# Feed-forward statistics and roots one step later in a run, and one more bank left out

## The chip, the core and the metric

The kernel runs on one core of a Trainium2 chip. The metric is the device time of one execution in microseconds (us). Five engines work side by side, each in its own program order: TensorE (PE, with its weight loads as PEld), VectorE (DVE), ScalarE (ACT), GpSimd (POOL) and SyncE (SP), which issues the DMAs. They wait for one another by semaphores.

## The reference

The input x is 2 x 256 x 128 x 128 (batch, time, band, channel), all float32. Three residual blocks follow each other:

```
x = x + mha(ln(x) over times, causal mask, 4 heads)     # sequences of 256 times
x = x + mha(ln(x) over bands, |i - j| <= 16, 4 heads)   # sequences of 128 bands
x = x + gelu(ln(x) @ w1.T + b1) @ w2.T + b2             # 128 -> 512 -> 128
```

`ln` subtracts the mean over the 128 channels and multiplies by one over the root of variance + 1e-5. `mha` has 4 heads of 32 channels.

## The kernel before, in words

**Groups and steps.** The work is cut into groups of 4 x 128 tokens (512 columns). `groups` (lines 953 to 1020) yields first 128 `OverTime` groups, which leave their results in HBM, then, in 16 runs, 8 `OverBands` groups and 8 `FeedForward` groups each (RUN = 32 times, NT = 4 a group). A run's feed-forward groups take the band groups' results from SBUF. "Run" in this document is always this; what is measured is called an execution. I call the band groups and their steps B0 to B7, the feed-forward ones F0 to F7. `run` (line 1143) is one loop over steps n, one group a step, in which pieces of neighbouring groups are issued in an order written out by hand. Every engine keeps that program order: `InOrder` (line 867) pins each instruction, and since its helper at line 877 emits them, the profile has this one line for all.

**One group's way through the steps.** Mean and variance ("statistics", lines 383 to 390, VectorE: four `bn_stats` to tile stats, four `bn_aggr` to mv); "root" (lines 399 to 403, GpSimd: a small add and a power, to rstd); "normalize" (VectorE, xh) and "turn" (VectorE's transpose to z, then four DMAs to HBM) in the step three before its own; "fetch" of the turned tile (xnT) two before its own.

- A band group has queries, keys and values (wf products) made one step before its own. In its step: scores (qT,kT) into four PSUM banks; a minimum and an add of the band mask on the fourth head by VectorE; four exps on ScalarE to tile pf; six masks on GpSimd for the first three heads ("first_mask", line 784). One step later: "weigh" (line 798), which sums the weights (pf,ones, to bank rp) and weighs the values (pf,v, to op); "invert" on ScalarE; "divide" on VectorE, to oT. Two steps later: "output" (wn,oT, to yp) and "finish", VectorE's add into x.
- A feed-forward group has hidden products (xnT,w1f) and gelus in its step, then one step later weigh (w2T, to zp) and VectorE's add into res with the store.

In F0, called "turn" in the code, the inversion is an exact reciprocal on VectorE instead. In feed steps GpSimd adds biases (res, x), and statistics, roots and, at the end, products of the next run's band groups are made.

**Order around the change.** FeedForward root of group n + 4 is the first thing issued in step n (line 1182), ahead of that step's six masks on GpSimd. FeedForward statistics of n + 5 stand at the end of VectorE's step, after divide, in band steps and F0 (line 1253), and in the other feed steps before weigh, right after normalize and turn (line 1240). So F0's statistics are in B3, F3's in B6, F4's in B7, F7's in F2, each with the root a step later.

**PSUM banks.** In the runs `turn_of_bank` (line 913) hands out the eight banks in turn. A matmul into a bank waits until the last reader of what was in it is done. `weigh` of a band group first takes a bank for each name in `follow` and holds it for use later in the same step (line 801): "yp" for the output of the group before, "qp" for the queries of the group two after. B0 to B5 have both names, B6 and B7 only "yp" (lines 1159 to 1161). Weigh of B5 is in step B6, weigh of B6 in step B7.

Of the kernel before, what the change touches and what calls it, by code (L numbers as in the profile page):

```python
# [636 lines left out]
class OverTime(Attention):  # L637
# [5 lines left out]
    early, late = (1, 2), (0, 3)  # L643
# [238 lines left out]
class BoundedPath:  # L882
# [260 lines left out]
    def run(self, x, out):  # L1143
        groups = list(self.groups(x, out))

        def do(n, *names):
            if 0 <= n < len(groups):
                for name in names:
                    getattr(groups[n], name)()

        def at(n, kind):
            return 0 <= n < len(groups) and isinstance(groups[n], kind)

        def do_at(n, kind, *names):
            if at(n, kind):
                do(n, *names)


        for i in range(len(groups) - 2):
            if at(i, OverBands) and at(i + 2, OverBands):  # L1160
                groups[i].follow = ("yp", "qp")

        run0 = [i for i in range(len(groups)) if at(i, OverBands)][: RUN // NT]
        times = range(3 * NT, run0[-1] + 1)
        fours = {i + NT - 1: Four(self, groups[i : i + NT]) for i in times[::NT]}
        A = RUN // NT

        ff = [i for i in range(len(groups)) if at(i, FeedForward)][2:]

# [5 lines left out]
        for n in range(-12, len(groups) + 2):  # L1175
# [3 lines left out]
            old, new = (groups[i] if at(i, OverTime) else None for i in (n, n + 1))  # L1179
            if bands[2] and feeds[1]:  # L1180
                self.scalar.preload_act_table_set(EXP_SET)
            do_at(n + 4, FeedForward, "root")
            do(n, "first_half", "first_function", "first_mask")
            if n >= 0:
                if n + 5 < 3 * NT:
# [51 lines left out]
            if n < 0:  # L1237
                do(n + 5, "statistics")
            if not bands[2] and not turn:
                do_at(n + 5, FeedForward, "statistics")  # L1240
            if n == -5:
                self.fold_biases()
            do(n - 1, "weigh")
# [6 lines left out]
                self.bounded = self.nc.values_load(self.flag[0:1, 0:1], min_val=0, max_val=1)  # L1250
            do(n - 1, "divide")
            if bands[2] or turn:
                do_at(n + 5, FeedForward, "statistics")
            if not turn:
                do(n, "second_half", "second_function")
            if n in run0:
# [1 line left out]
            if not bands[2] and old is None:  # L1258
                do_at(n, FeedForward, "bias")
                do_at(n + A, OverBands, "bias")  # L1260
                if at(n - 1, FeedForward) and at(n - 2, OverBands):
                    do_at(n + A - 1, OverBands, "statistics", "root")
                if not turn:
                    do_at(n + A, OverBands, "statistics", "root")
            do_at(n + 2, OverTime, "queries_keys", "take_query", "take_key")
# [99 lines left out]
```

## Time and profile before

| what | value |
|---|---|
| median of 3 timed executions | 2655.34 us (2655.3 to 2656.77) |
| the profiled execution | 2659.84 us |
| its span, first to last instruction | 2658.1 us |
| mean granted TensorE clock | 0.997 |
| one run, from B0's first weigh to the next run's | 106.22 us in most runs |
| TensorE idle over the runs (934 us to the end), gaps over 0.03 us | 10.5 us |

The page gives for each engine busy time, its share of the span and the number of instructions. A row of a timeline has the start in us from the beginning of the span, the length, engine, line, operation, tiles out<-in with shapes, the number of like instructions merged, and in brackets the idle time of the engine just before and what ended it. The chain of work is followed back from the last instruction, at each step to what released it.

### The profile page before, as it was taken

Reading aid. Unit: us, or ns where it says so; the run is one execution under the profiler, and the core shown is the slowest. Engines: PE = TensorE matmul, PEld = TensorE weight load, DVE = VectorE, ACT = ScalarE, POOL = GpSimd, SP = SyncE. Lnnn points to the kernel's source line nnn. Section 1 sums busy time; section 2 is a strip of 40 time slices with the busy share of each in tenths; the row PEclk is TensorE's granted clock in tenths of the full one; section 3 lists DMA queues with packets and bytes.
Section 4 is the critical chain, followed back from the end, with each engine's and each line's share of the span. In section 5 each row is a group of like instructions: output and inputs, shape, how many; then the busy total and the mean of one; then the engine's idle time right before and its main releaser. Section 6 shows DMA issues by size and latency. Waiting matters only on the chain.

```text
span 2658.1 us, 156476 instructions
## 1 busy us (share of the span) xinstructions
PE 2629.9 (99%) x68694; PEld 1924.4 (72%) x68694; DVE 2135.9 (80%) x6423; ACT 1843.1 (69%) x3562; POOL 1951.8 (73%) x2302
## 2 busy tenths in 40 slices
PE   8999999999999999999999999999999999999998
PEld 5676676676676667777777787777776867777777
DVE  6888888888888887967868779678687796886874
ACT  6889889989989874664755746647557466475573
POOL 5999999999999986766667667666676676666762
PEclk9999999999999999999999999999999999999999
DMA  5556565556566444544444445444454444444533
GB/s 136 146 152 156 144 159 151 149 152 152 148 156 153 126 121 121 126 122 123 120 122 123 120 120 126 120 123 120 117 130 122 115 128 122 124 118 122 126 94 83
DMA packets 469781, 344.97 MB, mean 130 GB/s; under 512 B 43104, under 2 KB 404448, under 8 KB 469088
## 3 DMA queue, kind: packets, MB, share of 16 engines
q1 hardware_dynamic: 467696, 333.82, 49.9%
q8 instruction: 540, 8.85, 1.5%
q14 instruction: 153, 1.25, 0.2%
q10 hardware_dynamic: 1392, 1.06, 0.1%
HBM read 167.98 MB, written 166.72 MB: 126 GB/s over the span
## 4 chain that ended last, share of the span: by engine, by line
PE 86%; DVE 12%; issue 0%; DMA 0%; ACT 0%; POOL 0%; SPq 0%; ACTq 0%; DVEq 0%
PE bank L877 86%; DVE xh L877 3%; DVE bank L877 2%; DVE u L877 1%; DVE oT L877 1%; DVE z L877 1%; DVE stats L877 1%; DVE x L877 1%; DVE mv L877 0%; DMA xnT<-turned 0%; ACT p L877 0%; DMA f_wiT_sb<-in_f_wiT 0%; DMA turned<-z 0%; POOL rstd L877 0%; POOL pf L877 0%
## 5 line engine op out<-in xcount | busy, mean ns | idle before, releaser
L877 ACT ACTIVATE hT<-bank,b 128x512 f32<-128x512 f32 x512 | 346.9, 688 | 522.4 <-PE bank L877 494.4
L877 POOL TENSOR_SCALAR_AFFINE_SELECT pf<-pf 128x512 f32<-128x512 f32 x768 | 476.7, 635 | 176.2 <-ACT pf L877 150.0
L877 PEld LDWEIGHTS bank<-w2T_sb,hT 128*32 128x32 f32 x16384 | 494.5, 110 | 27.6 <-issue 20.9
L877 PE MATMUL bank<-xnT,w1f 128*32 128x512 f32 x4096 | 507.3, 592 | 0.0
L877 PE MATMUL bank<-w2T_sb,hT 128*32 128x128 f32 x16384 | 502.1, 273 | 0.5 <-issue 0.3
L877 PE MATMUL bank<-xnT,wf 128*32 128x512 f32 x4096 | 498.0, 596 | 4.6 <-ACT p L877 3.9
L877 ACT ACTIVATE p<-bank 128x512 f32<-128x512 f32 (+1 forms) x1024 | 430.4, 495 | 64.7 <-PE bank L877 64.6
L877 POOL TENSOR_SCALAR_AFFINE_SELECT p<-p 128x1024 f32<-128x1024 f32 (+2 forms) x384 | 364.0, 948 | 84.8 <-ACT p L877 76.4
L877 DVE TENSOR_SCALAR xh<-x,mv,rstd 128x160 f32<-128x160 f32 (+1 forms) x1040 | 403.1, 430 | 9.6
L877 PEld LDWEIGHTS bank<-wf,xnT 128*32 128x32 f32 x8192 | 247.5, 110 | 142.4 <-issue 102.7
L877 DVE TENSOR_TENSOR res<-bank,res 128x512 f32<-128x512 f32 x256 | 170.6, 666 | 217.5 <-PE bank L877 203.4
L877 PEld LDWEIGHTS bank<-xnT,w1f 128*32 128x32 f32 x4096 | 239.7, 110 | 132.5 <-issue 116.7
L877 POOL TENSOR_TENSOR p<-p,p 128x512 f32<-128x512 f32 x256 | 323.8, 1287 | 10.7
L877 DVE BATCH_NORM_STATS2 stats<-x 128x6 f32<-128x128 f32 x1536 | 329.7, 277 | 0.6 <-DMA f_woT_sb<-in_f_woT 0.6
L877 POOL TENSOR_SCALAR rstd<-mv 128x4 f32<-128x4 f32 x248 | 56.6, 228 | 369.8 <-DVE mv L877 369.1
L877 PE MATMUL bank<-qT,kT 32*64 32x80 f32 (+4 forms) x16384 | 304.4, 271 | 1.6 <-ACT p L877 1.1
L877 PEld LDWEIGHTS bank<-qT,kT 32*64 32x64 f32 x16384 | 261.1, 131 | 53.4 <-ACT kT L877 50.0
L877 ACT ACTIVATE pf<-bank 128x512 f32<-128x512 f32 x512 | 267.7, 602 | 42.5 <-PE bank L877 33.2
L877 PE MATMUL bank<-wn,oT 128*32 128x128 f32 x8192 | 287.4, 274 | 1.8 <-issue 0.8
L877 DVE STREAM_TRANSPOSE z<-xh 128x512 f32<-128x512 f32 x380 | 270.5, 712 | 13.5
L877 PE MATMUL bank<-wf,xnT 128*32 128x128 f32 x8192 | 279.2, 273 | 0.0
L877 POOL TENSOR_TENSOR rstd<-rstd,mhalf 128x4 f32<-128x4 f32 x248 | 257.6, 1039 | 20.7
(99 smaller groups left out, 3826.5 us busy)
## 6 DMA issues: line engine op xcount, KB each, us to landing
turned<-z SPq DMA_DIRECT2D x1520, 64.0 KB, 2.6
xnT<-turned SPq DMA_DIRECT2D x380, 256.0 KB, 3.1
x<-res SPq DMA_DIRECT2D x256, 128.0 KB, 2.3
x<-x SPq DMA_DIRECT2D x128, 256.0 KB, 4.2
out<-res SPq DMA_DIRECT2D x256, 128.0 KB, 2.3
x<-in_x SPq DMA_DIRECT2D x124, 256.0 KB, 4.4
x<-in_x SPq DMA_DIRECT2D x8, 64.0 KB, 3.3
x<-in_x SPq DMA_DIRECT2D x4, 128.0 KB, 3.8
```

The lines of the kernel that those rows point to most:

```text
L877: return self.tc.keep_in_program_order(emit(*args, **kwargs))
```

## The change

Two edits, both in `run`.

1. `follow` gets "qp" where the next group is a band group, not the one two after. That adds B6: its weigh, in step B7, takes a bank for queries that nobody uses, so the turn of banks skips one there.
2. The first three feed-forward groups of a run (`early`) keep statistics five steps and root four steps ahead. The other five have both four steps ahead, at the place in the step where statistics stood, root right behind. So F3's statistics go from B6 to B7, F4's from B7 to F0, F5's to F1, F6's to F2, F7's to F3; and their roots go from the head of the same step to a place behind those statistics.

```
-            if at(i, OverBands) and at(i + 2, OverBands):
+            if at(i, OverBands) and at(i + 1, OverBands):
                 groups[i].follow = ("yp", "qp")
...
+        early = [i for i in range(3, len(groups)) if at(i, FeedForward) and at(i - 3, OverBands)]
+
+        def statistics_of_feed(n):
+            if n + 5 in early:
+                do(n + 5, "statistics")
+            if at(n + 4, FeedForward) and n + 4 not in early:
+                do(n + 4, "statistics", "root")
...
-            do_at(n + 4, FeedForward, "root")
+            if n + 4 in early:
+                do(n + 4, "root")
...
             if not bands[2] and not turn:
-                do_at(n + 5, FeedForward, "statistics")
+                statistics_of_feed(n)
...
             if bands[2] or turn:
-                do_at(n + 5, FeedForward, "statistics")
+                statistics_of_feed(n)
```

No instruction is added or taken away.

## The prediction

> **What bounds the kernel now.** I read the page first, then the chain of work that ended last, then the timelines of TensorE, GpSimd and VectorE around one run (the sixth of the sixteen, 1485.16 to 1591.38 us), then the same places in all runs. All instructions carry the helper's line L877, so I go by tiles.
>
> ```profile
> PE 2629.9 (99%) x68694; PEld 1924.4 (72%) x68694; DVE 2135.9 (80%) x6423; ACT 1843.1 (69%) x3562; POOL 1951.8 (73%) x2302
> ```
>
> TensorE is busy almost throughout, but a matmul's recorded length says little, so I take the starts of like blocks. The page *Perfetto Trace Analysis* of the Trainium skill, section Identifying the Most-Contended Engine, speaks against reading this 99% as a limit: matmul busy time is no measure of distance to roofline, weight loads (here 72%) are a better one. If TensorE had such room in the band steps, all VectorE time freed there would be time won.
>
> ```profile
> 1509.20 1.06 PE L877 MATMUL bank<-pf,ones 128*32 128x512 f32 x8
> ...
> 1515.43 1.21 PE L877 MATMUL bank<-pf,ones 128*32 128x512 f32 x8
> ...
> 1520.91 0.97 PE L877 MATMUL bank<-qT,kT 32*64 32x80 f32 x64
> 1522.38 1.07 PE L877 MATMUL bank<-pf,ones 128*32 128x512 f32 x8 [0.50 <-DVE oT L877]
> ...
> 1528.41 1.33 PE L877 MATMUL bank<-pf,ones 128*32 128x512 f32 x8
> ```
>
> The block "pf,ones" opens weigh once a band step. Its pitch is 6.23 us (1502.97 for B4, then 1509.20 and 1515.43), in nearly every run and band step. From B6 to B7 it is 6.95. Between scores and weigh lie 0.90 us normally (1508.30 to 1509.20), here 1.47: a loss of 0.57 us in B7, which waits for VectorE's oT. VectorE meanwhile:
>
> ```profile
> 1510.78 1.05 DVE xh L877 x3
> ...
> 1517.33 1.04 DVE xh L877 x3
> ...
> 1521.54 0.70 DVE oT L877
> 1522.24 0.14 issue
> 1522.38 7.64 PE bank L877 x124
> ```
>
> This is the chain. VectorE's step is 6.54 us from B3 on, without a gap, against TensorE's 6.23. It falls behind 0.31 us a step until in B7 TensorE has to wait for it. So the row decides against the skill's rule: TensorE kept 6.23 while VectorE was slower and not yet in its way. By the rule the freed 1.06 us a run would give 17 us; by the row only what TensorE lost can come back.
>
> Why does weigh wait for oT? The banks: B7's four score banks, yp, then rp. Without a "qp" between, rp takes the bank of the op that divide of B5's group reads, last of all VectorE work of that step. In B1 to B6, with "qp" reserved, rp takes a key bank that ScalarE emptied in the step before.
>
> The third view is GpSimd's.
>
> ```profile
> 1518.15 3.93 POOL L877 TENSOR_SCALAR_AFFINE_SELECT pf<-pf 128x512 f32<-128x512 f32 x6
> 1523.38 0.23 POOL L877 TENSOR_SCALAR rstd<-mv 128x4 f32<-128x4 f32 x1 [1.29 <-DVE mv L877]
> 1523.69 1.04 POOL L877 TENSOR_TENSOR rstd<-rstd,mhalf 128x4 f32<-128x4 f32 x1
> 1524.70 3.93 POOL L877 TENSOR_SCALAR_AFFINE_SELECT pf<-pf 128x512 f32<-128x512 f32 x6
> ```
>
> Each step's six masks stand behind a root that waits for VectorE's late statistics (1.29 us of idle before it). The first row is the masks of B6, to 1522.08; the last those of B7. They end at 1528.63, while F0's weigh begins at 1528.41: its column groups of the third and fourth head start 0.28 us after the first two. That lag is carried through the feed steps (mixed rows) and paid at the next scores: the last two w2T blocks stand 9.10 us apart in runs with it, 8.88 in the one run whose lag was 0.04. It costs 0.22 us. A run of 106.22 us thus loses 0.57 + 0.22 = 0.79, sixteen some 12 us.
>
> **The change, part by part.**
>
> *The bank.* rp of B6's group moves to the bank of the keys (copied by 1520.74), op to that of the values (1521.61), the four hidden banks of F0 to the four score banks (last read by exp at 1524.51, needed about 1527), yp to the bank of the yp before (read by 1526.70, needed at 1530). All are free in time. Weigh may start at 1520.91 + 0.90 = 1521.81. But the mask of the third head ends at 1522.08; its root is F2's, which does not move. With 0.06 for the handoff (1528.63 to 1528.69) the late groups start at 1522.14, not 1522.38. So the oT wait is gone, and a new lag of 0.33 takes part of its place.
>
> *Root of F3 leaves the head of B7.* The masks of B7 start with exp at about 1522.6 instead of 1524.70 and end near 1526.5, before F0's weigh at 1528.2. The old lag of 0.28 is gone. Together: the late groups reach F0's weigh at 1522.14 + 6.03 = 1528.17 where they had 1528.69. Gain 0.52 us a run, if VectorE keeps up. Here the skill speaks against it: *GPSIMD Engine Reference*, section 8 (Key points), says that GpSimd shares its SBUF interfaces with VectorE, and contends with VectorE instructions in a two-port mode or with two SBUF inputs. The masks now lie beside normalizing (1.60 us); were they held up for all of that, they would end at 1528.1, still in time. The trace shows 0.63 to 0.64 us a mask beside "xh" or not, so I take nothing.
>
> *Statistics.* Four BATCH_NORM_STATS2 and four aggregates cost 1.06 us of VectorE's queue (1522.14 to 1523.20). B6 loses one set, F3 gains one; B7, F0, F1 and F2 keep one, of the group before. In F3 it is covered by the wait for zp, 2.94 us a step in the timeline from F4 on. In B7 VectorE runs 1.06 earlier: minimum at 1522.14 (scores are ready at 1521.95), yp's add at 1525.02 (output ends 1524.95). No wait, but slack of only 0.2 and 0.1.
>
> *The new wait.* Statistics and normalize of F3 now stand back to back on VectorE over the step from B7 to F0, with GpSimd's root between; the same for F4 over F0 to F1. The trace has no such pair with GpSimd between. From below it is nothing, if other work stood between; here none does. From its rows: the last mv ends at 1523.29, the root at 1524.73, so 1.44, and 0.08 to VectorE; normalize used to start 0.08 before mv's end: 1.60 us each. I take that. Queued behind the first: turn, reciprocal, divide, and output of B7's group on TensorE.
>
> ```profile
> 1529.75 1.58 DVE L877 TENSOR_SCALAR xh<-x,mv,rstd 128x160 f32<-128x160 f32 x4
> ...
> 1531.99 3.32 DVE L877 RECIPROCAL ln<-bank 128x512 f32<-128x512 f32 x1
> ...
> 1536.49 0.43 DVE L877 TENSOR_SCALAR oT<-u 128x512 f32<-128x512 f32 x1
> ```
>
> oT ended at 1536.92; now 1536.92 - 1.06 + 1.60 = 1537.46, with 0.15 of handoff (1522.23 to 1522.38) 1537.61. TensorE's late groups wanted it at 1538.16, now 0.52 earlier: 1537.64. A tie: 0 to 0.1 us; I take 0.
>
> The second wait makes VectorE 0.54 + 1.60 = 2.14 late in F1. The add of zp would end at 1541.83 + 2.14 = 1543.97; the hidden product of F2 that reuses its bank starts about 1544.6. The last add of a band group ends at 1546.64; the zp that reuses its bank starts about 1546.95. Slack 0.5 and, after handoff, 0.16: nothing now, but tight. From F4 on VectorE has 2.94 us a step to catch up in. F5, F6 and F7 have no such wait: the add and the statistics of a later band group stand between theirs and their normalize.
>
> *GpSimd's queue.* Behind root F4 in F0 stand two bias adds, now from 1539.95 to 1542.5 instead of 1531.25 to 1533.77; the first is needed by the add at 1543.3. Covered. *SP's queue.* No DMA is added or passes another. z of F3 and F4 come 0.5 and 2.1 us later, as do the fetches behind them; F4's lands near 1549, wanted about 1552.5. Covered. ScalarE has no edit.
>
> **Sum.** Eleven runs like this: 11 x 0.52 = 5.7 us. The fifth loses 0.85 to oT and gains 0.81; the tenth, eleventh, twelfth and fourteenth have smaller waits: about 0.3, 0.25, 0.2 and 0.4. Together 7.7, less nothing for the tie. On the profiled execution, 2659.84 (span 2658.1 and 1.7 around it), that gives 2652.2; the median of the timed executions of before is 2655.34, 4.5 lower, and the same gain leads to 2647.7, say 2648.
>
> **Rivals.**
> 1. *The tie falls against it.* VectorE is 0.3 us later than worked out, and output of B7's group, or a bank in F2, pays for it. 16 x 0.3 = 4.8 of 7.7 go: 2652.5, no measurable change (within 0.2% is 5.3 us, about what a measurement can tell). For it: slacks of 0.03 and 0.16. Against it: durations repeat to 0.02 over the runs. Chance 0.26.
> 2. *Slower.* The 1.06 us is not banked, because VectorE in B7 waits for TensorE anyway. Then oT comes at 1536.92 + 1.60 + 0.15 = 1538.67 against 1537.64: 1.03 lost, 0.52 gained, 0.5 a run, 8 us: 2663. It decides once VectorE idles over 0.55 us in B7; I find slacks of 0.1 to 0.2 there. Chance 0.12.
> 3. *All of it returns.* If the mask of the third head came earlier too, 12 us: 2643. Its root is untouched. Chance 0.04.
>
> The forecast has 0.58. Faster by over 0.2%: 0.62; within: 0.26; slower: 0.12. The range from 2644.5 to 2656 leaves out rival 2 and part of rival 3.
>
> **What would show it.** Right: no idle of TensorE before "pf,ones" in B7 put down to oT, but third and fourth head 0.3 behind; masks of B7 ended two us before they are read; VectorE idle about 1.5 us before "xh" twice a run, put down to GpSimd's rstd; pitch of a run 105.7. Wrong: TensorE idle before "wn,oT" in F1, or before a "w1f" or "w2T" block in F2, for an add of VectorE.

## The result and the profile after

| what | before | after |
|---|---|---|
| median of timed executions (16 each) | 2655.94 us | 2651.66 us |
| lowest and highest | 2653.84, 2661.16 | 2646.06, 2655.38 |
| ratio, 95% interval | | 0.9982 [0.9975, 0.9989] |
| the profiled execution, its span | 2659.84, 2658.1 us | 2650.79, 2649.1 us |
| span from the first band weigh to the end | 1706.4 us | 1700.9 us |

The change made the kernel 4.8 us (0.18%) faster by the ratio (2.9 to 6.6); 7.7 were forecast. The two spans differ by 9.0 us, but 3.5 of these lie ahead of the first band weigh (951.74 against 948.19 us), where the program is the same. The four further traces begin that weigh at 947.7 to 949.4. The part that the change touches is 5.5 us shorter.

First the page's chain, which had 86% TensorE and 12% VectorE.

```profile
PE 97%; DVE 1%; ACT 0%; issue 0%; DMA 0%; POOL 0%; DVEq 0%; POOLq 0%; ACTq 0%
```

VectorE has left it. From the end of the tenth run's band steps into its feed steps, where the profile shows none of the irregular stalls of which more below, the chain is one piece:

```profile
1904.99 55.11 PE bank L877 x1429
```

TensorE's timeline of the same place, with scores of B7, weigh in B7, weigh in F0 and output of B7's group in F1:

```profile
1935.48 1.22 PE L877 MATMUL bank<-pf,ones 128*32 128x512 f32 x8
...
1940.96 0.97 PE L877 MATMUL bank<-qT,kT 32*64 32x80 f32 x64
1941.86 1.38 PE L877 MATMUL bank<-pf,ones 128*32 128x512 f32 x8
...
1947.92 1.35 PE L877 MATMUL bank<-pf,ones 128*32 128x512 f32 x8
...
1957.57 1.14 PE L877 MATMUL bank<-wn,oT 128*32 128x128 f32 x30
```

No idle stands before weigh in B7 any more: 0.90 us from scores to weigh (1940.96 to 1941.86), where it was 1.47. But the block lasts 1.38 instead of 1.07. Its third and fourth head start 0.32 us after the first two, because the mask of the third head ends at 1942.13, the end of B6's six masks (first row of the next view). That lag was forecast as 0.33, and F0's weigh carries it on. GpSimd and VectorE at the same place:

```profile
1938.20 3.93 POOL L877 TENSOR_SCALAR_AFFINE_SELECT pf<-pf 128x512 f32<-128x512 f32 x6
1942.64 3.93 POOL L877 TENSOR_SCALAR_AFFINE_SELECT pf<-pf 128x512 f32<-128x512 f32 x6 [0.51 <-ACT pf L877]
1948.92 0.23 POOL L877 TENSOR_SCALAR rstd<-mv 128x4 f32<-128x4 f32 x1 [2.35 <-DVE mv L877]
1949.24 1.04 POOL L877 TENSOR_TENSOR rstd<-rstd,mhalf 128x4 f32<-128x4 f32 x1
```

```profile
1947.70 0.86 DVE L877 BATCH_NORM_STATS2 stats<-x 128x6 f32<-128x128 f32 x4
1948.48 0.36 DVE L877 BATCH_NORM_AGGREGATE mv<-stats 128x2 f32<-128x6 f32 x4
1950.31 1.61 DVE L877 TENSOR_SCALAR xh<-x,mv,rstd 128x160 f32<-128x160 f32 x4 [1.48 <-POOL rstd L877]
...
1952.59 3.32 DVE L877 RECIPROCAL ln<-bank 128x512 f32<-128x512 f32 x1
...
1957.09 0.43 DVE L877 TENSOR_SCALAR oT<-u 128x512 f32<-128x512 f32 x1
...
1960.05 1.61 DVE L877 TENSOR_SCALAR xh<-x,mv,rstd 128x160 f32<-128x160 f32 x4 [1.47 <-POOL rstd L877]
```

B7's masks now wait for ScalarE's exps alone and are done at 1946.57, over a microsecond before F0's weigh. The two new waits of VectorE, for the roots of F3 and F4, are there in every run, 1.48 and 1.47 us of idle. oT ends at 1957.52 and output starts at 1957.57: the tie.

**A run's account.** For each kernel I took the pitch of the weigh blocks on TensorE, step by step, and its excess over the shortest pitch that this step has in any run but the last. In the trace of after these shortest pitches add up to 105.24 us a run; I take that as the floor for all kernels. A run in which TensorE has no irregular stall (a "regular" run; in after the third, fifth and tenth) stands above that by:

| kernel | regular run over its floor |
|---|---|
| before | 0.98 us |
| after | 0.46 us |

The difference of 0.52 us is the forecast's, to the hundredth; a regular run of after takes 105.70 us, 105.7 were forecast. Irregular stalls are gaps like this one of after, in B6 of its sixth run, behind which the profile shows no releaser:

```profile
1513.25 0.52 PE L877 MATMUL bank<-pf,v 128*32 128x128 f32 x9 [0.70 <-issue]
```

They hit a few other places in each execution.

### The profile page after: what moved, and what is told of

Its sections match the earlier page's. It is cut to its first block, busy times and chain, and to the rows that moved or that the text cites. A ratio compares the mean times of both kernels' runs of the same rounds, so it can differ in the third digit from the quotient of the medians.

```text
span 2649.1 us, 156479 instructions
## 1 busy us (share of the span) xinstructions
PE 2626.7 (99%) x68694; PEld 1871.0 (71%) x68694; DVE 2141.1 (81%) x6423; ACT 1842.9 (70%) x3562; POOL 1950.7 (74%) x2302
## 3 DMA queue, kind: packets, MB, share of 16 engines
q14 instruction: 153, 1.25, 0.2%
q10 hardware_dynamic: 1392, 1.06, 0.1%
## 4 chain that ended last, share of the span: by engine, by line
PE 97%; DVE 1%; ACT 0%; issue 0%; DMA 0%; POOL 0%; DVEq 0%; POOLq 0%; ACTq 0%
PE bank L877 97%; DVE stats L877 0%; DVE xh L877 0%; ACT p L877 0%; DVE ln L877 0%; ACT hT L877 0%; DVE z L877 0%; DMA xnT<-turned 0%; DVE u L877 0%; DVE bank L877 0%; DVE res L877 0%; DVE oT L877 0%; DVE mv L877 0%; DVE x L877 0%; POOL rstd L877 0%
## 5 line engine op out<-in xcount | busy, mean ns | idle before, releaser
L877 PEld LDWEIGHTS bank<-w2T_sb,hT 128*32 128x32 f32 x16384 | 476.0, 110 | 49.0 <-issue 22.7
L877 PE MATMUL bank<-xnT,w1f 128*32 128x512 f32 x4096 | 496.1, 592 | 0.0
L877 PE MATMUL bank<-w2T_sb,hT 128*32 128x128 f32 x16384 | 490.8, 273 | 1.4 <-issue 0.7
L877 PEld LDWEIGHTS bank<-xnT,w1f 128*32 128x32 f32 x4096 | 206.1, 110 | 154.9 <-issue 88.4
```

Source lines behind the costliest of these rows:

```text
L877: return self.tc.keep_in_program_order(emit(*args, **kwargs))
```

## The experiments

All four were timed on one other chip, where before has a median of 2657.65 us.

### The changed kernel again

No edit.

> The changed kernel once more, for comparison with the others on the same chip. My theory: a regular run is 0.52 us shorter than before (0.46 us over its floor instead of 0.98), and the irregular stalls of TensorE that the profile puts down to issue, absorbed before by the wait for oT in B7, are now paid. So 7 to 8 us in an execution without such stalls, about 4.5 to 5 in the usual one: ratio 0.998 to 0.9985. Rival (gain of the same 5 us, but the tie at output of B7's group takes what is missing): a regular run would be only 0.3 us shorter.

Ratio 0.9979 [0.9970, 0.9988], median 2652.13 us. The 0.46 us over the floor come again, but only in two of the inner fourteen runs, the seventh and tenth, and these have short stalls of 0.16 and 0.27 us that cost nothing (more on this below); from the first band weigh to the end it took 1702.0 us. So the size of the gain and the size of the saving in a regular run repeat, against the rival.

### The bank alone

```
-            if at(i, OverBands) and at(i + 2, OverBands):
+            if at(i, OverBands) and at(i + 1, OverBands):
```

> Before with the bank edit alone. My theory: the wait for oT in B7 is gone and the first two column groups start weigh 0.57 us earlier, but the masks of B7 still stand behind F3's root, so the third and fourth head of F0's weigh start where they did: lag 0.85 us there instead of 0.28, paid at the next scores. Gain 0 to 1 us, ratio 1.000. Rival (the bank is the whole of the change): 0.3 to 0.5 us a run, 5 to 8 us, ratio 0.997 to 0.998.

Ratio 1.0001 [0.9992, 1.0010]. A regular run stands 0.97 us over the floor, as before. TensorE and GpSimd, sixth run:

```profile
1518.15 0.97 PE L877 MATMUL bank<-qT,kT 32*64 32x80 f32 x64
1519.05 1.38 PE L877 MATMUL bank<-pf,ones 128*32 128x512 f32 x8
...
1525.11 1.44 PE L877 MATMUL bank<-pf,ones 128*32 128x512 f32 x6
...
1526.38 0.60 PE L877 MATMUL bank<-pf,ones 128*32 128x512 f32 x2
```

```profile
1520.62 0.23 POOL L877 TENSOR_SCALAR rstd<-mv 128x4 f32<-128x4 f32 x1 [1.29 <-DVE mv L877]
1520.93 1.04 POOL L877 TENSOR_TENSOR rstd<-rstd,mhalf 128x4 f32<-128x4 f32 x1
1521.94 3.93 POOL L877 TENSOR_SCALAR_AFFINE_SELECT pf<-pf 128x512 f32<-128x512 f32 x6
```

Weigh in B7 follows scores after 0.90 us, so the wait for oT is gone. But the masks of B7 end at 1525.87. In F0's weigh the third and fourth head start 0.82 us after the first two (0.85 expected), and the last two of the eight instructions start only at 1526.38. All that was won in B7 is lost: 0.43 us in the pitch behind F0's weigh and 0.10 more at the run's end. The rival, that the bank is the change, falls.

### The statistics and roots alone

```
-            if at(i, OverBands) and at(i + 1, OverBands):
+            if at(i, OverBands) and at(i + 2, OverBands):
```

This is against the changed kernel.

> The changed kernel without the bank edit. My theory: weigh in B7 still waits 0.57 us for oT (statistics come after it on VectorE), but the masks of B7 are early and the lag of 0.28 us at F0's weigh is gone: 0.22 us a run, 3.5 us, ratio 0.9987. No wait at output of B7's group, as TensorE is later. Rival (the two back-to-back waits for the root, 1.5 us each, cost more than the freed statistics give): slower, 0.3 us a run or more, ratio 1.002.

Ratio 0.9995 [0.9986, 1.0004]: no difference that this measures. A regular run stands 0.71 us over the floor, 0.27 less than before (0.22 expected). The wait in B7 is still there, the lag in F0 is not (1.07 us for the block, no late head):

```profile
1520.20 1.07 PE L877 MATMUL bank<-pf,ones 128*32 128x512 f32 x8 [0.49 <-DVE oT L877]
...
1526.24 1.07 PE L877 MATMUL bank<-pf,ones 128*32 128x512 f32 x8
```

VectorE's waits of 1.48 and 1.47 us are there, and oT of B7's group still comes 0.20 us before output starts. So the rival, slower by these waits, falls. Fifteen times 0.27 would be 4 us; from the first band weigh on, the trace has 0.6 (1705.7 against 1706.4). The other stalls took the rest: 1.3 us more in the first run (0.99 of it from the test told below), 1.2 more in the feed steps of the others, 0.7 more of what irregular stalls in B2 to B6 cost.

The parts alone bring 0.01 and 0.27 us in a regular run, together 0.52. Each removes one of two waits for the same late VectorE that stand one behind the other.

### The reciprocal ahead of F3's normalize

```
+            if turn:
+                do(n - 1, "weigh", "invert_exactly")
             do_at(n + 3, (OverBands, FeedForward), "normalize", "turn")
...
-            do(n - 1, "weigh")
-            do(n - 1, "invert_exactly" if turn else "invert")
+            if not turn:
+                do(n - 1, "weigh", "invert")
```

This is on top of the changed kernel.

> The changed kernel with weigh and reciprocal of B7's group issued ahead of normalize and turn of F3 in F0, so that the reciprocal (3.3 us of VectorE) fills the wait for F3's root. My theory: VectorE's idle of 1.48 us before normalize of F3 goes, oT of B7's group comes over 0.5 us before TensorE wants it, and the 0.07 to 0.13 us lost at output in F1 return: 1 to 2 us less than the changed kernel. Rival (the tie costs more than I think, 0.2 us a run): over 3 us less. Rival (xnT of F3 is turned 2 us later and TensorE waits for it in F3): slower than the changed kernel.

Ratio 0.9969 [0.9957, 0.9980], median 2649.23 us of six executions. VectorE in its twelfth run:

```profile
2159.43 3.36 DVE L877 RECIPROCAL ln<-bank 128x512 f32<-128x512 f32 x1 [0.49 <-PE bank L877]
2162.71 1.51 DVE L877 TENSOR_SCALAR xh<-x,mv,rstd 128x160 f32<-128x160 f32 x4
...
2166.17 0.43 DVE L877 TENSOR_SCALAR oT<-u 128x512 f32<-128x512 f32 x1
```

The wait for F3's root is filled, and oT comes 0.96 us before output starts instead of 0.05. In F1 the excess of 0.14 us, which a regular run of the changed kernel has there, is gone. But a regular run stands 0.46 us over the floor, as in the changed kernel. At the run's end, where queries and scores bring the column groups together, the excess is 0.32 us now, 0.17 in the changed kernel. While TensorE waited for oT, the leading column groups stood and the late ones caught up: the tie paid a part of the lag early and cost nothing of its own. So my 1 to 2 us from the tie fall, and the rival's 3 too. The median is 2.9 us below the changed kernel's on that chip, the intervals overlap, and only a part can be put down to the edit: in the trace the first run has 1.0 us less than in after, 0.91 of it where the once-only test stands (told below), and the other runs have fewer stalls. The rival that F3 waits for its turned tile falls too: the kernel isn't slower.

### What was not run

Two kernels would have settled more. One issues the roots of F0 to F2 behind the step's masks, which should remove the remaining lag of 0.32 us. The other adds a stall of known size to TensorE in B5, with and without the change.

## Why the prediction was right, and where it was not

The direction was right and 2651.66 lies in the range. The gain was given too large, 7.7 against 4.8 us; measured 0.18% lies within the 0.2% to which the prediction gave a chance of only 0.26.

**Right, with sizes.** The bank ends the wait for oT (0.57 us; none left). Masks behind F2's root leave a lag in B7: 0.33 said, 0.32 measured. The lag at F0 from F3's root goes. VectorE's 1.06 us is banked in B7: no idle until the root. The root's wait is 1.60 us from back to back; 1.48 of idle plus the overlap that normalize had before. oT against output was called a tie; it starts 0.05 after. The saving in a regular run is 0.52. The contention of GpSimd with VectorE, for which the prediction cites the Trainium skill (*GPSIMD Engine Reference*, section 8, Key points), did not show where the prediction looked for it: 3.93 us for six masks beside normalize, as before. It showed in the first run.

**Where it failed: the sum over the runs.** "Together 7.7, less nothing for the tie" takes 0.52 us for eleven runs, the first and the last among them, and for the other five what their waits in the trace of before leave to gain. It asks neither what is different in the first run nor why some waits were smaller. From the first band weigh to the end, the change against before in us:

| part | after | after, again |
|---|---|---|
| inner fourteen runs, as regular ones | -7.2 | -7.2 |
| the same runs, irregular stalls in the band steps | +1.2 | +1.9 |
| the same runs, irregular stalls in the feed steps | +1.1 | +1.0 |
| first run, its own saving included | +0.7 | +1.1 |
| last run | -1.3 | -1.1 |
| together | -5.5 | -4.3 |

So the step that failed is this sum, not the saving in a run. Two of its terms are told here.

*The first run.* In its F2 and F3 stands a once-only test of the weights: VectorE multiplies gs, and ScalarE may overwrite gs only then. In program order gelus of the next groups stand behind that on ScalarE. Counted from the run's first weigh, VectorE starts the first multiply of the test 2.14 us later than in before, as much as the forecast gave the two waits for roots. The multiply then also lasts longer, 1.29 us instead of 0.28, because it now starts beside a bias add of GpSimd. VectorE in before, VectorE in after, GpSimd in after:

```profile
1016.80 0.28 DVE L877 TENSOR_TENSOR gs<-gs 128x128 f32<-128x128 f32 x1
```

```profile
1015.39 1.29 DVE L877 TENSOR_TENSOR gs<-gs 128x128 f32<-128x128 f32 x1
```

```profile
1015.26 1.28 POOL L877 TENSOR_TENSOR res<-x,rows_sb 128x512 f32<-128x512 f32 x1
```

In the four traces in which the statistics are moved this multiply lasts 1.28 or 1.29 us; in before and with the bank alone, where it meets only the last 0.14 us of an add, 0.28. In all six traces both multiplies of the test end 0.15 us after a bias add of GpSimd has ended. Their two inputs lie in SBUF, the case that the section of the skill cited above names. ScalarE in before, then in after:

```profile
1017.12 0.31 ACT L877 ACTIVATE gs<-wf 128x128 f32<-128x128 f32 x1 [2.72 <-DVE gs L877]
...
1017.86 1.25 ACT L877 ACTIVATE hT<-bank,b 128x512 f32<-128x512 f32 x2
```

```profile
1016.72 0.31 ACT L877 ACTIVATE gs<-wf 128x128 f32<-128x128 f32 x1 [6.38 <-DVE gs L877]
...
1017.46 2.40 ACT L877 ACTIVATE hT<-bank,b 128x512 f32<-128x512 f32 x4
```

The last number is how long ScalarE stood: 6.38 against 2.72 us. In before two gelus were ready behind the test, in after all four, and the next weigh, which needs them, lasts 4.78 us on TensorE (1018.18 to 1022.96) instead of 3.74. From the weigh of F2's group to that of F4's TensorE's excess in this run is 0.74 us in before and 0.84 with the bank alone; with the statistics moved it is 1.87 (after), 1.85 (its repeat) and 1.73 (statistics alone): 1.1 us once. With the reciprocal first it is 0.96 again. The forecast listed GpSimd's and SP's queues behind the late VectorE and missed ScalarE's.

*Irregular stalls.* In before a stall of TensorE in B2 to B6 was mostly free: weigh in B7 had to wait for oT anyway and waited less. After the change a regular run has only 0.46 us left over its floor that could shrink in this way, so a longer stall is paid for the most part. These are all inner runs with more than 0.6 us of stalls from weigh in B2 to weigh in B6 and no further stall up to F1, with what these runs took over a regular one (the cost of stalls in later feed steps taken off):

| kernel | stalls, us | paid, us |
|---|---|---|
| before | 0.70, 0.79 | 0.07, 0.13 |
| bank alone | 0.86, 0.93, 0.93 | 0.30, 0.16, 0.41 |
| statistics alone | 0.67, 0.72, 1.18 | 0.27, 0.47, 0.66 |
| after | 0.96, 0.93 | 0.59, 0.92 |
| after, again | 0.63 | 0.49 |

Shorter stalls stayed mostly free: in the traces of after, its repeat and the reciprocal first, fifteen runs had 4.6 us of them and paid 1.0. So a run with a long stall gains less than 0.52. That absorption is the reason is argued from these few runs; no run imposed a stall of known size. Executions of after scatter somewhat more, with a standard deviation of 2.6 us on both chips against 1.9 and 2.0 for before. Why stalls in the feed steps cost about 1 us more in both traces of after stays open.

What makes the stalls no run varied, but the DMA packets in the traces point to TensorE's own instructions. Of the packets of 16 KB on the instruction queue q8 one starts about every 4.9 us. In the six traces TensorE has, from the first band weigh on, 37 gaps over 0.04 us that are put down to issue. Every one ends 1.27 to 1.63 us after the end of such a packet; of matmuls without idle before them about one in fifteen starts at that distance. The three gaps of 0.39 to 0.76 us put down to ScalarE's pf in B4 of the eighth run lie alike (1.25 to 1.31 us). Why these packets come too late stays open.

**The rivals.** The first, the tie falling against it, has the size nearly right (2652.5) but not the mechanism: with the reciprocal first the tie has 0.9 us of slack and regular runs don't change. The second, slower by a VectorE that can't bank its 1.06 us, did not happen. What the prediction drew from the skill's caution against the 99%, that all VectorE time freed would come back, did not hold either: 1.06 us came back as 0.52. The caution itself, that matmul busy time doesn't measure the distance to roofline, no run here tests.

## What to carry to other kernels

When an engine is late, look for all that waits for it, one behind the other: here a PSUM bank in one step and, through GpSimd, the masks in the next, and removing the first alone brought nothing. A regular stretch times its count is not yet the gain, since a wait that is removed had also absorbed stalls that are now paid. And before an operation is made late, look through every queue behind it for work done only once, ScalarE's here, and for what it will newly stand beside.

## What the runs showed of the hardware

TensorE's four column groups of 128x32 weights run apart. When the third head's mask was 0.3 us late, the groups of the first two heads went on and kept that lead through some 55 us of feed steps (mixed rows in the timeline), until queries and scores brought them together: 0.32 us of excess there without a wait between, 0.17 with one. A wait in between takes the lead away and costs only what exceeds it.

A VectorE multiply of two 128x128 tiles of SBUF took 1.28 or 1.29 us when it started just behind a GpSimd add of 1.28 us, and 0.28 when it met only the last 0.14 of one, while six GpSimd masks took 3.93 us beside normalize and without it.
